# Cross-attention on one core: how Wq and Wk reach TensorE, and when x is loaded

## The chip, the core and the metric

The kernel runs on one core of a Trainium2 chip. The core has five engines that run side by side and wait for one another through semaphores: TensorE (PE in the profile, its weight loads PEld), VectorE (DVE), ScalarE (ACT), GpSimd (POOL) and SyncE (SP), which here issues every DMA. TensorE reads SBUF and writes PSUM, which has eight banks; VectorE and ScalarE copy results from PSUM to SBUF. The metric is device time in microseconds (us), as the median of the runs.

## The reference

One cross-attention layer with a residual and a layer norm. x is 16 x 256 x 256, the context c is 16 x 77 x 192; there are 8 heads of 256.

```
Q = (x @ Wq).reshape(B, -1, H, D).transpose(0, 2, 1, 3)     # Wq: 256 x 2048
K = (c @ Wk).reshape(B, -1, H, D).transpose(0, 2, 1, 3)     # Wk: 192 x 2048
V = (c @ Wv).reshape(B, -1, H, D).transpose(0, 2, 1, 3)     # Wv: 192 x 2048
score = jnp.einsum('bhqd,bhkd->bhqk', Q, K) / math.sqrt(D)
score = jnp.where(mask, score, -jnp.inf)
attn = jax.nn.softmax(score, axis=-1)
ctx = jnp.einsum('bhqk,bhkd->bqhd', attn, V).reshape(B, -1, H * D)
out = ctx @ Wo + x                                          # Wo: 2048 x 256
mu, var = mean and variance of out over its last axis
return (out - mu) * jax.lax.rsqrt(var + EPS) * gamma + beta
```

All of it is float32.

## The kernel before, in words

The weights of each head are multiplied with each other first, so that Q, K and V are never formed. For head h, G_h = Wk_h Wq_h^T / sqrt(D) is 192 x 256 (tiles gA for the first 128 rows, gB for the last 64), and U_h = Wv_h Wo_h is 192 x 256 (uA, uB). Then, for a group of four batches, A = G_h^T c^T (tile a, 256 x 77 for each head and batch), scores are x A, and for a batch V' = c U_h (tile vw, with the last 13 keys in vr). The keys are cut at 64 and 77.

The order on every engine is the order of the text: nothing is reordered by a planner. There are two stages.

The *opening* (lines 430 to 622) runs once, in this order on TensorE:

- `keep_busy(10)`: idle transposes of the identity.
- the c rows are turned by TensorE (line 475, tile pc), evicted by ACT and DVE to cA and cB; POOL doubles cB's half (line 486) and makes cRA, cRB, then clears vr (487 to 490).
- for each head, `turn_qk` turns its columns of Wq (two chunks of 128 rows) and Wk (two chunks of 96 rows) by four TensorE transposes each (line 507, tiles p_wqT and p_wkT), so that the head dimension lies on partitions; ACT evicts the one, DVE the other.
- pg (line 543) is a head's G for the first 128 rows, ph (line 524) a pair's last 64 rows, two heads side by side in the array.
- `prepare_a(0, ...)` makes A of the first group in two halves of four heads: part_A (line 182) with gA and cA, part_B (line 196) with gB and cB. Its eight banks are evicted by ACT and DVE in turn. After each half DVE turns two of the four wvT tiles by blocks of 32 x 32 (line 568).
- pu and pw (584, 602) make U, with two 64-row halves of the array at once; ACT and DVE evict, POOL copies uB's other half (613).
- pr (256, 266) makes the last keys' values; DVE turns the first group's xT; POOL turns the mask into bias (572, 618).

The loads go out in one queue on SP, in the order of the text: c in three pieces, then for each head 1-kB pieces of Wq and of Wk, then Wv in sixteen pieces of 96 KB (blocks: 32 rows on 32 partitions), Wo, the mask, xT of the first group (x in blocks), then x itself, all four groups of 1 MB (line 129; tile xg, in memory that the turned weights held before), gamma and beta. At most eight loads are under way: a load waits for the eighth before it. Any load waits in this queue behind the ones before it.

The *loop* (633 to 685) has one pass per batch: scores (295), mask and softmax on DVE, POOL and ACT, vw of the next batch (223, 234), a quarter of A of the next group (182, 196), attend (360), and finish, which adds x (372), takes the statistics and normalises; the result is stored from xg. At the first pass of a group `load_xT` loads x in blocks for the next group.

Of the kernel before, what the change touches and what calls it, by code (L numbers as in the profile page):

```python
# [15 lines left out]
P = 128  # L16
# [28 lines left out]
def kernel(  # L45
# [16 lines left out]
    LP = DL // 2  # L62
# [34 lines left out]
    gA = const.tile([P, H, DI], F32, tag="gA", name="gA")  # L97
    gB = const.tile([P, NF, DI], F32, tag="gB", name="gB")
# [66 lines left out]
    def prepare_a(g, pairs, B_first=False):  # L165


        if 0 in pairs:
            a_of[g] = in_two("a", [P, 2, GB, H, S2], g)
        parts = [(2 * n + i, dc) for n in pairs for dc in range(2) for i in range(2)]  # L170
# [19 lines left out]
        def part_B():  # L190
            if B_first:
                banks.extend(ring_of(parts))
            for j in range(0, len(parts), 2):
                for i in range(NM):
                    for k, (h, dc) in enumerate(parts[j : j + 2]):
                        nc.tensor.matmul(  # L196
                            flat(banks[j + k][i * BK : (i + 1) * BK]),
                            gB[half(k), h // 2, cols(dc, i)],
# [233 lines left out]
    with tc.tile_pool(name="wonce", bufs=1) as wp:  # L432
        c_sb = wp.tile([CR, NCR, DL], F32, tag="c", name="c_sb")
        wq_r = wq.rearrange("(t p) f -> p t f", p=P)
        wk_r = wk.rearrange("(t p) f -> p t f", p=LP)

        warm = wp.tile([P, 1], F32, tag="warm", name="warm")
        nc.scalar.activation(warm, eps, AF.Exp)
        wq_all = wp.tile([P, NF, 2, 2 * D], F32, tag="w128", name="wq_all")
        wk_all = wp.tile([LP, NF, 2, 2 * D], F32, tag="w96", name="wk_all")  # L440
        for lo, hi in ((0, 2), (2, 6), (6, NCR)):
            nc.sync.dma_start(c_sb[:, lo:hi, :], c_rows[:, lo:hi, :])
        for h in range(H):
            here, cols = slice(h % 2 * D, (h % 2 + 1) * D), slice(h * D, (h + 1) * D)
            nc.sync.dma_start(wq_all[:, h // 2, :, here], wq_r[:, :, cols])
            nc.sync.dma_start(wk_all[:, h // 2, :, here], wk_r[:, :, cols])

        wvT = wp.tile([P, NF, NL, P], F32, tag="wvT", name="wvT")
        wo_all = wp.tile([P, NF, 4, DI], F32, tag="w128", name="wo_all")
        wv_blocks = wv.rearrange("(m r) (a i f) -> a i r m f", r=BK, a=NF, i=NM)  # L450
        wo_rows = wo.rearrange("(a p n) f -> a p n f", p=P, n=4)
        for a in range(NF):
            for i in range(NM):
                nc.sync.dma_start(wvT[i * BK : (i + 1) * BK, a], wv_blocks[a, i])
        for a in range(NF):
            nc.sync.dma_start(wo_all[:, a], wo_rows[a])
# [12 lines left out]
        keep_busy(10)  # L469
        for r in range(0, NCR, 2):  # L470
            n = min(2, NCR - r)
            pc = ps_mm.tile([P, 4, P], F32, tag="mm", name=f"pc_{r}")
            for lc in range(2):
                for j in range(n):
                    nc.tensor.transpose(  # L475
                        pc[:, 2 * lc + j, :CR],
                        c_sb[:, r + j, lc * LB : lc * LB + P],
                        ident[:CR, :CR],
                    )
            rows = slice(r * CR, (r + n) * CR)  # L480
            evacuate(flat(cA)[:, rows].rearrange("p (j m) -> p j m", m=CR), pc[:, :n, :CR])
            evacuate(
                flat(cB)[LB:, rows].rearrange("p (j m) -> p j m", m=CR),
                pc[LB:, 2 : 2 + n, :CR],
            )
            nc.gpsimd.tensor_copy(flat(cB)[:LB, rows], flat(cB)[LB:, rows])
        nc.gpsimd.tensor_copy(cRA, cA[:, :, KM:])
        nc.gpsimd.tensor_copy(cRB, cB[:, :, KM:])

        nc.gpsimd.memset(vr, 0.0)  # L490


        wqT_of = [
            const.tile([P, H // 2, 2, DI], F32, tag=f"xg{i}", name=f"wqT_{i}") for i in range(2)
        ]
        wkT_of = [
            const.tile([P, H // 2, 2, DL], F32, tag=f"xg{i + 2}", name=f"wkT_{i}") for i in range(2)
        ]
        wqT = [wqT_of[h * 2 // H][:, h % (H // 2)] for h in range(H)]
        wkT = [wkT_of[h * 2 // H][:, h % (H // 2)] for h in range(H)]  # L500

        def turn_weight(dst, w_all, rows, h, tag):
            pt = ps_mm.tile([P, 4, P], F32, tag="mm", name=f"p_{tag}_{h}")
            for dc in range(2):
                for r in range(2):
                    lo = h % 2 * D + dc * P
# [222 lines left out]
```

## Time and profile before

| | us |
|---|---|
| median of 3 runs | 288.12 (287.86 to 289.52) |
| the profiled execution | 290.4 |
| its span, first to last instruction | 288.2 |
| opening, until the first scores | 61.5 |
| first pu matmul starts | 41.0 |
| TensorE busy | 277.7 (96%) |
| VectorE busy | 212.9 (74%) |
| GpSimd, ScalarE busy | 119.3, 118.5 (41% each) |
| bytes moved by DMA | 22.5 MB |

The span is the profiled execution without what lies before its first and after its last instruction, here 2.2 us. TensorE's busy time counts a matmul from its start to a modelled end. PEclk is the clock that TensorE was granted, as a share of its full speed. A group's row gives its line, engine and operation, what it writes and reads, its shape, how many there were, busy time and mean duration of one. In the chain of work, a row is when a piece starts, how long it lasts and what it is. One float32 matmul counts as two in the trace, a transpose as one.

### The profile page before, as it was taken

The numbers are of one execution on the slowest core, as the hardware profiler recorded it, in microseconds if no ns is written. First come the engines' busy times: TensorE is split into PE (matmuls) and PEld (weight loads), VectorE is DVE, ScalarE is ACT, GpSimd is POOL, SyncE is SP. The second block draws the span as 40 slices with busy tenths as digits, with TensorE's granted clock in tenths as the row PEclk, the third lists the DMA queues.
The fourth block names the chain that finished last, engine by engine and source line by source line (L and its number), as shares of the span: only waits on it lengthen the run. The fifth ranks groups of instructions, "written<-read, shape, count | busy, mean of one in ns | idle before, by whom it ended". The sixth has DMA issues, their size and how long they took to land.

```text
span 288.2 us, 11524 instructions
## 1 busy us (share of the span) xinstructions
PE 277.7 (96%) x5216; PEld 182.9 (63%) x5216; DVE 212.9 (74%) x419; ACT 118.5 (41%) x205; POOL 119.3 (41%) x150
## 2 busy tenths in 40 slices
PE   5999999999999999999999999999999999999990
PEld 5877569994757575757575757475757467575550
DVE  1322383755858798989797989897979898898884
ACT  3343221122353535353535353535353525635541
POOL 2700050705443424253434252534342518658484
PEclk9799999999999999999999999999999999999997
DMA  7998998991000100900000009000001010010112
GB/s 198 242 227 182 349 194 235 342 179 15 5 3 2 37 8 30 156 28 13 25 20 23 18 18 166 17 30 9 32 8 36 5 37 9 32 41 3 39 37 74
DMA packets 34673, 22.50 MB, mean 78 GB/s; under 512 B 17648, under 2 KB 33984, under 8 KB 34624
## 3 DMA queue, kind: packets, MB, share of 16 engines
q1 hardware_dynamic: 34624, 21.77, 32.6%
q8 instruction: 41, 0.67, 1.0%
q14 instruction: 8, 0.07, 0.1%
HBM read 17.57 MB, written 4.19 MB: 76 GB/s over the span
## 4 chain that ended last, share of the span: by engine, by line
PE 92%; DMA 2%; DVE 2%; POOL 2%; issue 1%; ACT 0%; POOLq 0%; SPq 0%
PE ps L295 23%; PE po L360 22%; PE pa L182 12%; PE pv L223 10%; PE pa L196 6%; PE pv L234 6%; PE pu L584 3%; PE pg L543 2%; PE pr L256 2%; DMA c_sb<-in_ctx_dram 2%; PE p_wqT L507 2%; PE ph L524 1%; PE pw L602 1%; PE p_wkT L507 1%; PE pr L266 1%; PE pc L475 1%
## 5 line engine op out<-in xcount | busy, mean ns | idle before, releaser
L317 POOL TENSOR_TENSOR s<-s,top 128x616 f32<-128x616 f32 x32 | 38.9, 1217 | 90.9 <-DVE top L316 86.4
L295 PE MATMUL ps<-a,xT 128*32 128x154 f32 x2048 | 70.0, 294 | 0.0
L295 PEld LDWEIGHTS ps<-a,xT 128*32 128x32 f32 x2048 | 66.4, 110 | 3.5 <-issue 0.7
L338 POOL TENSOR_TENSOR p<-e,rden 128x512 f32<-128x512 f32 x64 | 50.1, 802 | 31.8 <-ACT a L667 27.0
L360 PE MATMUL po<-vw,pT 128*32 128x256 f32 x1024 | 61.5, 380 | 0.0
L360 PEld LDWEIGHTS po<-vw,pT 128*32 128x32 f32 x1024 | 31.8, 110 | 28.2 <-issue 5.5
L330 DVE TENSOR_REDUCE den<-e 128x8 f32<-128x616 f32 x32 | 25.3, 790 | 23.6 <-ACT e L324 23.6
L182 PE MATMUL pa<-cA,gA 128*32 128x308 f32 x512 | 35.8, 423 | 0.0
L324 ACT ACTIVATE e<-s 128x616 f32<-128x616 f32 x32 | 23.0, 719 | 28.7 <-POOL s L317 28.7
L665 ACT COPY vw<-pv 128x512 f32<-128x512 f32 x32 | 18.6, 581 | 36.2 <-PE pv L234 36.2
L309 DVE TENSOR_TENSOR s<-ps,bias 128x308 f32<-128x308 f32 x64 | 27.8, 466 | 4.1 <-PE ps L295 4.1
L223 PE MATMUL pv<-uA,cA 128*32 128x512 f32 x256 | 30.4, 592 | 0.0
L182 PEld LDWEIGHTS pa<-cA,gA 128*32 128x32 f32 x512 | 16.4, 110 | 21.0 <-issue 6.6
L417 DVE SCALAR_TENSOR_TENSOR xg<-xg,rstd,bet 128x256 f32<-128x256 f32 x25 | 27.9, 1116 | 0.9
L385 ACT ACTIVATE std<-mv,eps 128x2 f32<-128x2 f32 (+1 forms) x17 | 5.0, 296 | 55.0 <-DVE mv L377 54.3
L348 DVE STREAM_TRANSPOSE pT<-p 128x640 f32<-128x640 f32 x32 | 25.0, 810 | 2.5 <-POOL p L338 2.5
L316 DVE TENSOR_REDUCE top<-s 128x8 f32<-128x616 f32 x32 | 25.5, 796 | 1.1
L360 PE MATMUL po<-vr,pT 128*32 128x256 f32 x256 | 19.7, 379 | 0.0
L385 ACT ACT_TABLE_LOAD x15 | 19.2, 1283 | 0.3
L196 PE MATMUL pa<-cB,gB 64*32 64x308 f32 x512 | 19.3, 419 | 0.0
L324 ACT ACT_TABLE_LOAD x14 | 18.0, 1283 | 0.2
L234 PE MATMUL pv<-uB,cB 64*32 64x512 f32 x256 | 17.4, 601 | 0.0
(73 smaller groups left out, 282.0 us busy)
## 6 DMA issues: line engine op xcount, KB each, us to landing
xT<-in_x_dram SPq DMA_DIRECT2D x16, 256.0 KB, 7.4
xg<-in_x_dram SPq DMA_DIRECT2D x4, 1024.0 KB, 11.4
out_dram<-xg SPq DMA_DIRECT2D x15, 256.0 KB, 2.2
wq_all<-in_L_xattn_Wq_dram SPq DMA_DIRECT2D x8, 256.0 KB, 7.7
wo_all<-in_L_xattn_Wo_dram SPq DMA_DIRECT2D x4, 512.0 KB, 5.8
wk_all<-in_L_xattn_Wk_dram SPq DMA_DIRECT2D x8, 192.0 KB, 7.7
wvT<-in_L_xattn_Wv_dram SPq DMA_DIRECT2D x16, 96.0 KB, 3.7
bias<-in_mask_BxS_if_dram SPq DMA_DIRECT2D x1, 616.0 KB, 9.3
```

Of the source, the lines that this page charges most:

```text
L182: nc.tensor.matmul(flat(o[i * BK : (i + 1) * BK]), gA[:, h, cols(dc, i)], flat(cA[:, batches, :]), start=not B_first, stop=B_first,)
L196: nc.tensor.matmul(flat(banks[j + k][i * BK : (i + 1) * BK]), gB[half(k), h // 2, cols(dc, i)], flat(cB[half(k), batches, :]), start=B_fir ...
L223: nc.tensor.matmul(pv[k][i * BK : (i + 1) * BK], cA[:, b, k * BK : (k + 1) * BK], uA[:, :, :, i], start=True, stop=False,)
L234: nc.tensor.matmul(pv[k][i * BK : (i + 1) * BK], cB[half(k), b, k * BK : (k + 1) * BK], uB[half(k), :, :, i], start=False, stop=True,)
L295: nc.tensor.matmul(ps[m // 2][i * BK : (i + 1) * BK, m % 2 * 2 * S2 : (m % 2 + 1) * 2 * S2], xT_of[g][:, j * NM + m, dc], flat(a_of[g][:, ...
L309: nc.vector.tensor_tensor(s[:, a * H // 2 : (a + 1) * H // 2], ps[a][:, : H // 2 * S2].rearrange("p (h k) -> p h k", k=S2), bias[:, b, :]. ...
L316: nc.vector.tensor_reduce(top, s, AX.X, ALU.max)
L317: nc.gpsimd.tensor_tensor(s, s, top.unsqueeze(2).to_broadcast([P, H, S2]), ALU.subtract)
L324: nc.scalar.activation(e, s_of.pop(t), AF.Exp)
L338: nc.gpsimd.tensor_tensor(part, e_mh[:, :, :, keys], rden_mh.unsqueeze(3).to_broadcast(list(part.shape)), ALU.mult,)
L360: nc.tensor.matmul(po[i * BK : (i + 1) * BK], pT[:, n, i], vw_of[b][:, n // 2, n % 2, :] if n < NF else vr[:, b, :], start=(n == 0), stop= ...
L417: nc.vector.scalar_tensor_tensor(y, y, rstd, bet, ALU.mult, ALU.add)
```

## The change

Heads are taken by two numbers: head = 2a + half in pairs before, and now place u (0 to 3) and e (0 or 1), head = u + 4e.

1. The first load is no longer c. Wq and Wk of the heads with u = 0 and 1 are loaded in pieces of 2 kB (two heads of a row), on all 128 partitions: Wk's first 128 rows for e = 0, its last 64 rows as 128 half rows, Wq for e = 0, then Wk and Wq for e = 1. They are turned by TensorE, in sets of four 128 x 128 transposes.
2. Then come three of the eleven c row sets (`first`), and the other four heads (u = 2 and 3) in blocks: each load puts 32 rows on 32 partitions in pieces of 512 bytes, as was done for Wv. VectorE turns these by 32 x 32 blocks (`turn_blk`), and G for them is made with `of_pair` and `rest_of_pairs`, the functions that pu and pw now use too.
3. A of the first group is made in two parts with G of the block heads between: places 0 and 1 after the first G, places 2 and 3 after the second. The remaining c rows are loaded after the blocks and turned after A; so POOL's cRA, cRB and vr come later too.
4. DVE turns three of the wvT tiles before the second part's copies of A and the last after them.
5. x of a group is loaded in the loop, right behind xT of that group; only x(0) is loaded in the opening, together with gamma and beta.
6. Fourteen idle transposes at the start, and two and three more between the first sets. Wo has two tiles; the second lies in wq_nat's memory, the first in its own.

```diff
-    def prepare_a(g, pairs, B_first=False):
-        if 0 in pairs:
...
-                            gB[half(k), h // 2, cols(dc, i)],
+                            gB[half(k), h % NF, cols(dc, i)],
...
-        wq_r = wq.rearrange("(t p) f -> p t f", p=P)
-        wk_r = wk.rearrange("(t p) f -> p t f", p=LP)
...
+        wq_nat = wp.tile([P, 2, 2, 2 * D], F32, tag="w128", name="wq_nat")
+        wk_nat = wp.tile([P, 2, 2 * D], F32, tag="wk", name="wk_nat")
+        wk_last = wp.tile([P, 2 * D], F32, tag="wl", name="wk_last")
...
+        wq_blk = wp.tile([P, 2, DI // BK, P], F32, tag="wqb", name="wq_blk")
+        wk_blk = wp.tile([P, 2, NL, P], F32, tag="wkb", name="wk_blk")
+        wq_blocks = wq.rearrange("(m r) (a i f) -> a i r m f", r=BK, a=NF, i=NM)
...
+        wq_rows = wq.rearrange("(t p) (e f) -> e p t f", p=P, e=2)
+        wk_rows = wk[:P].rearrange("p (e f) -> e p f", e=2)
+        wk_ends = wk[P:].rearrange("r (e f) -> (r e) f", e=2)
...
+        def load_blocks(to, blocks):
+            for i in range(NM):
+                nc.sync.dma_start(to[i * BK : (i + 1) * BK], blocks[i])
+        def load_c(lo, hi):
+            nc.sync.dma_start(c_sb[:, lo:hi, :], c_rows[:, lo:hi, :])
+        first = -(-GB * S2 // CR)
+        nc.sync.dma_start(wk_nat[:, 0], wk_rows[0][:, : 2 * D])
+        nc.sync.dma_start(wk_last, wk_ends[:, : 2 * D])
+        nc.sync.dma_start(wq_nat[:, 0], wq_rows[0][:, :, : 2 * D])
+        nc.sync.dma_start(wk_nat[:, 1], wk_rows[1][:, : 2 * D])
+        nc.sync.dma_start(wq_nat[:, 1], wq_rows[1][:, :, : 2 * D])
+        load_c(0, first)
+        for e in range(2):
+            load_blocks(wk_blk[:, e], wk_blocks[2 * e + 1])
+            load_blocks(wq_blk[:, e], wq_blocks[2 * e + 1])
+        load_c(first, NCR)
...
-        wq_all = wp.tile([P, NF, 2, 2 * D], F32, tag="w128", name="wq_all")
-        wk_all = wp.tile([LP, NF, 2, 2 * D], F32, tag="w96", name="wk_all")
-        for lo, hi in ((0, 2), (2, 6), (6, NCR)):
-            nc.sync.dma_start(c_sb[:, lo:hi, :], c_rows[:, lo:hi, :])
-        for h in range(H):
-            here, cols = slice(h % 2 * D, (h % 2 + 1) * D), slice(h * D, (h + 1) * D)
-            nc.sync.dma_start(wq_all[:, h // 2, :, here], wq_r[:, :, cols])
-            nc.sync.dma_start(wk_all[:, h // 2, :, here], wk_r[:, :, cols])
...
+        wo_of = [
+            wp.tile([P, 2, 4, DI], F32, tag=tag, name=f"wo_{i}") for i, tag in enumerate(("wo", "w128"))
+        ]
...
-            for i in range(NM):
-                nc.sync.dma_start(wvT[i * BK : (i + 1) * BK, a], wv_blocks[a, i])
+            load_blocks(wvT[:, a], wv_blocks[a])
         for a in range(NF):
-            nc.sync.dma_start(wo_all[:, a], wo_rows[a])
+            nc.sync.dma_start(wo_of[a // 2][:, a % 2], wo_rows[a])
...
-        keep_busy(10)
...
+        keep_busy(14)
...
+        qT = const.tile([P, 2, 2, 2, DI], F32, tag="xg0", name="qT")
+        kT = const.tile([P, 2, 2, 2, DL], F32, tag="xg2", name="kT")
+        qT_blk = const.tile([P, 2, 4, DI], F32, tag="xg1", name="qT_blk")
+        kT_blk = const.tile([P, 2, 4, DL], F32, tag="xg3", name="kT_blk")
...
+        def turn_q(e, u):
+            chunks = [
+                wq_nat[:, e, t, u * D + dc * P : u * D + (dc + 1) * P]
+                for dc in range(2) for t in range(2)
+            ]
+            pt = turn_chunks(chunks, f"q_{e}_{u}")
+            evacuate(flat(qT[:, e, u]), flat(pt))
+        def turn_k(e):
+            pt = turn_chunks([wk_nat[:, e, n * P : (n + 1) * P] for n in range(4)], f"k_{e}")
             evacuate(
-                flat(cB)[LB:, rows].rearrange("p (j m) -> p j m", m=CR),
-                pc[LB:, 2 : 2 + n, :CR],
+                kT[:, e].rearrange("p u n l -> p (u n) l")[:, :, :P], pt
             )
...
+        def turn_k_last():
+            pt = turn_chunks([wk_last[:, n * P : (n + 1) * P] for n in range(4)], "kl")
+            for e in range(2):
+                evacuate(
+                    kT[:, e].rearrange("p u n l -> p (u n) l")[:, :, P:],
+                    pt.rearrange("p n (r e) -> p e n r", e=2)[:, e],
+                )
+        def turn_blk(e):
+            for blk, of in ((wk_blk, kT_blk), (wq_blk, qT_blk)):
+                nc.vector.transpose(
+                    of[:, e].rearrange("p n (m r) -> p m n r", r=BK),
+                    blk[:, e].rearrange("p m (n c) -> p m n c", c=BK),
+                )
+        def turn_c(lo, hi):
...
+                nc.gpsimd.tensor_copy(flat(cB)[:LB, rows], flat(cB)[LB:, rows])
...
+        def of_pair(out, a, weight, moving):
...
             for n in range(4):
                 for e in range(2):
                     nc.tensor.matmul(
-                        pu[e][:, a % 2, :],
-                        wv_part(a, e, n)[:, :P],
-                        wo_all[half(e), a, n, :],
+                        out[e][:, a % 2, :],
+                        weight(a, e, n)[:, :P],
+                        moving(a, e, n),
                         start=(n == 0),
                         stop=(n == 3),
                     )
...
+        def rest_of_pairs(j, pairs, weight, moving, name):
+            banks = [ps_mm.tile([P, DI], F32, tag="mm", name=f"{name}_{j}_{e}") for e in range(2)]
             for n in range(4):
-                for i in range(2):
+                for i, a in enumerate(pairs):
                     for e in range(2):
                         nc.tensor.matmul(
-                            pw[e][half(i)],
-                            wv_part(pair + i, e, n)[:, P:],
-                            wo_all[half(e), pair + i, n, :],
+                            banks[e][half(i)],
+                            weight(a, e, n)[:, P:],
+                            moving(a, e, n),
                             start=(n == 0),
                             stop=(n == 3),
                         )
+            return banks
...
+        def wq_part(a, e, n):
+            return qT_blk[half(e), a, n]
+        def wk_part(a, e, n):
+            return kT_blk[half(e), a, n]
...
+        def g_of(e):
...
+            pg = ps_mm.tile([P, 2, DI], F32, tag="mm", name=f"pg_{e}")
+            for u in range(2):
+                for dc in range(2):
+                    nc.tensor.matmul(
+                        pg[:, u],
+                        kT[:, e, u, dc, :P],
+                        qT[:, e, u, dc],
+                        start=(dc == 0),
+                        stop=(dc == 1),
+                    )
+            nc.scalar.mul(gA[:, NF * e : NF * e + 2], pg, D ** -0.5)
...
+        def a_of_places(places, between=None):
+            part_A, part_B, copies = prepare_a(0, places)
+            part_A()
+            part_B()
+            for i, (dst, src) in enumerate(copies()):
+                evacuate(dst, src)
+                if between and i == 3:
+                    between()
+        turn_k(0)
+        keep_busy(2)
+        turn_k_last()
+        keep_busy(3)
+        turn_q(0, 0)
+        turn_q(0, 1)
+        g_of(0)
+        turn_k(1)
+        turn_q(1, 0)
+        turn_q(1, 1)
+        g_of(1)
+        rest_of_g(0)
+        rest_of_g(1)
+        turn_c(0, first)
+        turn_blk(0)
+        a_of_places((0, 1), lambda: turn_blk(1))
+        pg = two_banks("pgb", 0)
+        for e in range(2):
+            of_pair(pg, e, wk_part, wq_part)
+        for i in range(2):
+            nc.scalar.mul(gA.rearrange("p (e u) d -> p u e d", e=2)[:, 2 + i], pg[i], D ** -0.5)
+        for i, ph in enumerate(rest_of_pairs(0, (0, 1), wk_part, wq_part, "phb")):
+            nc.vector.tensor_scalar(gB[:, 2 + i, :], ph, D ** -0.5, None, ALU.mult)
+        for a in range(3):
+            turn_v(a)
+        load_x(0)
+        nc.sync.dma_start(gam, gamma.partition_broadcast(P))
+        nc.sync.dma_start(bet, beta.partition_broadcast(P))
+        a_of_places((2, 3))
+        turn_v(3)
+        turn_c(first, NCR)
+        nc.gpsimd.tensor_copy(cRA, cA[:, :, KM:])
+        nc.gpsimd.tensor_copy(cRB, cB[:, :, KM:])
+        nc.gpsimd.memset(vr, 0.0)
...
-        for g in range(NG):
-            load_x(g)
-            if g == 0:
-                nc.sync.dma_start(gam, gamma.partition_broadcast(P))
-                nc.sync.dma_start(bet, beta.partition_broadcast(P))
-        for n in range(0, NF, 2):
-            part_A, part_B, copies = prepare_a(0, (n, n + 1), B_first=(n > 0))
-            for part in (part_A, part_B)[:: -1 if n else 1]:
-                part()
-            for dst, src in copies():
-                evacuate(dst, src)
-            for a in range(n, n + 2):
-                blocks = wvT[:, a].rearrange("p m (c n) -> p m n c", n=4)
-                nc.vector.transpose(blocks, blocks)
...
@@ -654,6 +740,7 @@
             work.append(prepare_a(g, (n,)))
             if n == 0:
                 load_xT(g)
+                load_x(g)
```

The turned weights lie in the memory of x: qT in that of xg0, qT_blk in xg1, kT in xg2, kT_blk in xg3.

## The prediction

> **What bounds the kernel now.** I read the page's busy shares first, then the chain of work that ended last, then the stretches of the opening, then the groups for durations. Busy shares and granted clock, from the page:
>
> ```profile
> PE 277.7 (96%) x5216; PEld 182.9 (63%) x5216; DVE 212.9 (74%) x419; ACT 118.5 (41%) x205; POOL 119.3 (41%) x150
> ```
>
> TensorE is busy almost throughout. The chain in order of time (start, length, what) says whether it ever waits:
>
> ```profile
> 1.66 5.46 DMA c_sb<-in_ctx_dram
> ...
> 7.17 1.62 PE pc L475 x10
> 8.79 0.85 PE p_wqT L507 x4
> ...
> 16.38 0.45 PE p_wqT L507 x4
> 16.83 0.07 issue
> 16.89 0.52 PE p_wkT L507 x4
> 17.41 0.89 PE pg L543 x4
> 18.31 1.88 PE ph L524 x16
> ...
> 28.15 4.28 PE pa L182 x64
> 32.43 4.31 PE pa L196 x128
> 36.74 4.28 PE pa L182 x64
> 41.02 7.77 PE pu L584 x64
> ```
>
> From 7.17 on the chain is TensorE work, unbroken to 271. After 61.5 come the loop passes (14.49 us each while A is made for a later group, 11.37 after that), whose work on TensorE the change leaves alone. So I need one number: when the first pu matmul starts, 41.02 now. Busy times by stretch (start:end, length, PE busy, PEld, DVE, ACT, POOL, granted clock, DMA share, GB/s):
>
> ```profile
> 6.00:8.00 2.00, 0.83 (x7) 0.84 (x8) 0.61 (x2) 0.38 (x2) 0.74 (x2) 0.94 1.08 262
> 8.00:10.00 2.00, 2.00 (x13) 1.99 (x11) 0.98 (x3) 1.07 (x4) 1.02 (x4) 0.50 1.12 242
> 12.00:14.00 2.00, 1.96 (x14) 1.60 (x13) 0.67 (x2) 0.58 (x1) 2.00 (x1) 1.00 1.13 238
> 24.00:28.00 4.00, 4.00 (x29) 2.60 (x27) 0.98 (x2) 1.36 (x3) 0.00 (x0) 1.00 0.61 165
> ```
>
> Two things: the weights arrive at 238 to 242 GB/s, and the clock is halved around 9 us, after the 1.37 us gap before 7.17.
>
> **What goes from TensorE.** Full-clock costs are the chain's: a 128-row Wq set of four transposes 0.45, a 96-row Wk set 0.33, one head's pg 0.89, four pairs of ph 3.76. Before: transposes 8x(0.45+0.33)=6.24, pg 8x0.89=7.12, ph 3.76. After: natural transposes 4 sets of Wq and 3 of Wk (two plus the last rows), all of 128 columns, 7x0.45=3.15; pg of four heads 3.56, ph 1.88; the other four heads as of_pair on two 64-row halves at once. Those have pu's shape: 7.77/4=1.94 a pair, 3.88; their rest has pw's (chain: 3.67 for four pairs), 1.84. Total 17.12 becomes 14.31: 2.8 us less work. The rest of the gain must come from waits and the half clock: before spends 28.15-8.79=19.36 on those 17.12.
>
> **The opening, rebuilt.** Nothing of c is needed now before the weights. Bytes start to move near 2.1 (first issue 0.72). Landing lags moving: c's 0.95 MB had landed at 7.12, when the stretch 0 to 7.2 had moved 198x7.2=1.43 MB. I take 0.45 MB of lag at 1-kB pieces, somewhat less early. The first three loads, 1.05 MB, free the first turn_q. The 2-kB strided piece is in no row; bounds are 240 GB/s (1-kB pieces of the same rows) and 394 (4-kB pieces of Wo, stretch 32 to 36); nearest is the first, I take 300. With 1.4 MB moved: 2.1+1.4/0.3 = 6.8, say 7.0 (6.0 to 7.8). Before that TensorE has 14 idle transposes at 0.22 (ends 4.4) and then 5 idle and 8 real ones at 0.11: done near 5.9, so the nine added idle ones cost nothing unless the load lands before that. From T=7.0: two Wq sets 0.9, wait for the second copy 0.55 (a 512-column eviction is 0.58 on ACT, 0.69 on DVE), pg 1.78, Wk set 0.45: T+3.7. The second half of Wq (1.84 MB landed, 2.3 moved: 9.8) is there by then, so TensorE sets the pace. Two sets 0.9, wait 0.4, pg 1.78, ph 1.88, six c transposes 0.6, their copies 0.5 (0.35 and 0.25 on ACT), first A 4.28+2.15, pgb and phb 5.72, second A 6.43, the other sixteen c transposes 1.6 (four of 96 columns are 0.33, of 128 columns 0.45, so 0.4 at 112): 26.2. Sum: pu starts at 7.0+3.7+26.2=36.9, 4.1 earlier.
>
> **What must hide beside it.** *VectorE's block turns.* Two per half, 768 and 1024 columns. Two rows bound them: pT (whole 32-column blocks moved, as here) 128x640 in 0.81, so 2.3 us a half; wvT, interleaved by four, 128x768 in 1.63, so 3.8. I take the first. The first half runs from T+10, beside A's 6.4; the second is queued after four of A's eight copies, near T+15.6, ends T+17.9 and is wanted at T+18.1 by pgb's second pair (by the wvT price 1.3 us of stall). Behind it on VectorE stand two copies of A, whose banks are wanted 3 us later: nothing. *Landing of the blocks.* Sixteen loads of 96 and 128 KB, 1.84 MB. Here the Trainium skill speaks against the change: "DMA: Bandwidth & Descriptors", Rules for kernel authors, asks for at least 1 MiB a load, and its Bandwidth section gives 138 GB/s at 64 KB. By that figure they take 13.3 us after the c rows (landed near 11.5), the second half lands near 24.8, is turned at 27.1 and wanted at 25.1: 2 us of stall. The row that resembles them is Wv, the same 512-byte pieces in 96-KB loads: 3.7 us to landing with eight in flight, 8x98 kB/3.7 = 212 GB/s. By it 8.7 us: landed near 20.2, VectorE free for it at 22.6. I go by the row, the same pieces and sizes. *Queues.* SP issues 23 loads ahead of Wv where it issued 19, 0.3 to 0.5 us each, faster than they land; bytes ahead of Wo are the same, so Wo lands no later than now. The second Wo tile waits for TensorE's last read of wq_nat, 15 us earlier than SP gets there. x(1) to x(3) go onto SP behind xT of their group, 1.76 us of issue each; only stores stand behind them, and those wait 187 us for DVE anyway; each is needed four passes (58 us) later against 11.4 to land. Without that cover one wait would show in DVE's first addition. *DVE and POOL behind A.* turn_c's rest now follows turn_v(3), and VectorE has from 28.9 on two gB 0.85, three wvT turns 4.9, four copies of A 1.9, the fourth turn 1.6, four cB 1.6: until 39.8. POOL's last cB copy, cRA, cRB (0.37 each), vr memset 3.51 and bias 4.38 follow and end near 48.8. The six uB copies that pr's second part needs (0.40 each) then end near 51.2; TensorE wants them at 36.9+7.77+3.67+3.01=51.35. A tie; between 0 and 1 us I charge 0.2. ACT has room.
>
> **The clock.** The new opening leans on transposes to keep the clock up. The skill's "TensorE: Matmul & The Clock Gate", Part 4, says that transposes don't raise it. By that rule pg of the first four heads and the sets between run at half speed, some 2.5 us more, and the gain is 1.5. The trace contradicts it: the ten opening transposes go at 0.22 us each (1.34 to 3.53), the eight c ones at 4.81 at about 0.1, with no other matmul before. So transposes do raise it here, and the gap before 7.17 took it away again: by one-microsecond stretches (0.88 from 7, 0.92 from 11) the half clock lasted from 7.76 to 11.16, and in the 3.4 us before it TensorE was busy for 1.6. In the new opening that stretch holds 2.3 us of work, with a gap of about 1 us. Whether that suffices no row tells: a half clock there costs 1.4 (in before it hid behind the weights, which paced TensorE until 16.89).
>
> **The sum.** 288.2-4.1+0.2=284.3 of span. The profiled execution took 290.4, 2.2 outside the span: 286.4 for one like it. The runs' median is 288.12, close to the span itself: 284.2. One per cent, 2.9 us, is about what can be told from no change here, since repeats differ by 0.6%.
>
> **The rivals.**
> A. As summed, clock kept: 284.2 (283.2 to 285.8 by the bounds of landing and of the tie on POOL). Chance 0.52.
> B. The clock drops in the opening: the gap of about 1 us and the row at 8 to 10 speak for it, the higher busy share against: 4.1-0.2-1.4, 285.6. Chance 0.26.
> C. The blocks or the block turns come late (the 138 GB/s, the wvT price): 1.3 to 3.3 us of stall before pgb's second pair, 285.5 to 287.5. Chance 0.12.
> D. Slower: the first five loads. All take 2 kB out of every 8-kB row, and if such pieces draw on few of memory's channels at a time, the second Wq half decides in place of TensorE. From T4, its landing, pu is 26.2 away; equal to now at T4=14.8, which is 2.3 MB in 12.7 us, 180 GB/s; at 145 GB/s T4 is 18 and the time 291.3. For it: the strided 1-kB pieces got 240 where 4-kB ones got 394. Against: the same rows never fell below 199 in stretches that were not starved of issues. Chance 0.07.
> E. The loop gives it back (x loads against xT and stores): DMA share there is 0.16, so 0.03, near 288.
>
> **How the numbers follow.** A's time is the prediction. 282.8 to 286.9 holds A, B and most of C. Under 285.2 is faster by over 1%: most of A (0.49), two fifths of B (0.10), little of C (0.03): 0.62. Within: 0.31, with E. Slower, from D: 0.07.
>
> **What would show it.** Right: first pu matmul near 37; no DMA wait before TensorE after the second Wq half; idle before pgb's second pair under 0.3; block turns 1.0 and 1.3 us; loop passes still 14.49; granted clock 1.0 from about 4. Wrong: first turn_q later than 8, a clock of 0.5 near 8 to 11, wk_blk or wq_blk as releaser of DVE with pgb waiting for it, POOL's uB holding pr by more than 1 us.

## The result, and the profile after

| | before | after |
|---|---|---|
| median of 20 runs | 289.35 (287.86 to 292.71) | 286.38 (285.98 to 289.17) |
| median span of the runs | 287.2 (32 runs beside the first experiments) | 284.6 (20 runs) |
| outside the span, median | 2.15 | 1.79 |
| the profiled execution, its span | 290.4, 288.2 | 285.98, 284.2 |
| first pu matmul starts | 41.02 | 36.82 |
| from there to the end of the span | 247.2 | 247.4 |

The kernel became faster by 0.9%: the ratio is 0.991, with a 95% interval of 0.9893 to 0.9928. Ratios here leave out the runs that are over 1.5% longer than the fastest of their kernel, and they are not the quotient of the two medians, which is 0.990. The gain is clear of noise; the one per cent that the prediction took as its bound lies inside the interval. The forecast was 284.2, in a range of 282.8 to 286.9. The range holds the result; the number is 2.2 us too low, and case A's own range (to 285.8) misses the result by 0.6.

The three runs that the prediction started from (289.52, 287.86 and 288.12) are the first three of these 20; their median, 288.12, lies 1.2 us below that of all 20.

Busy times, from the page of the changed kernel:

```profile
PE 274.4 (97%) x5221; PEld 180.2 (63%) x5221; DVE 215.3 (76%) x421; ACT 115.2 (41%) x199; POOL 119.1 (42%) x150
```

TensorE is busy for 3.3 us less than in the profiled execution before, VectorE for 2.4 us more. The chain of work of the changed kernel, in order of time (start, length, what):

```profile
1.34 3.25 PE idle L493 x14
4.59 0.85 PE pt_k L507 x4
...
5.74 0.43 PE pt_kl L507 x4
6.17 0.33 PE idle L493 x3
6.50 0.62 PE pt_q L507 x4
...
7.98 1.96 PE pg L611 x8
9.94 0.44 PE pt_k L507 x4
10.38 0.45 PE pt_q L507 x4
...
16.49 4.35 PE pa L184 x64
20.84 2.23 PE pa L198 x64
23.08 3.65 PE pgb L568 x32
...
35.14 1.68 PE pc L545 x16
36.82 7.77 PE pu L568 x64
```

No DMA is in it: TensorE begins the first Wq sets at 6.50, goes into the second half's at 10.38 (that half had landed at 10.04), runs without a pause from A (16.49) through the block heads' G (pgb) and the second A, and starts pu at 36.82. The forecast was 36.9. Before, this was 41.02.

Four stretches of the opening (start:end, length, PE, PEld, DVE, ACT, POOL, granted clock, DMA share, GB/s):

```profile
6.00:8.00 2.00, 1.56 (x14) 1.17 (x12) 1.12 (x2) 0.86 (x3) 0.00 (x0) 1.00 0.98 321
8.00:10.00 2.00, 2.00 (x11) 1.75 (x11) 0.00 (x0) 0.18 (x2) 0.00 (x0) 1.00 1.18 247
12.00:14.00 2.00, 2.00 (x13) 1.40 (x14) 0.00 (x0) 0.48 (x1) 0.00 (x0) 1.00 0.98 195
18.00:20.00 2.00, 2.00 (x36) 1.03 (x32) 1.03 (x1) 0.00 (x0) 0.00 (x0) 1.00 1.06 240
```

Between 6 and 8 the 2-kB pieces arrive at 321 GB/s, where the old order had 262; the blocks come at 195 to 240 later. The clock at 8 to 10, which was 0.50, is 1.00. (A row prints 1.00 also for the time before a trace's first record of the clock, which lies at 5.46 us here and at 4.34 in the profile before. In that time the speed has to be read from the transposes: 0.22 us each at first, 0.11 from 5.74 on.)

The two closest waits of the changed kernel, from its timeline (start, length, engine, line, operation, in brackets an engine's idle time and what released it):

```profile
23.46 1.20 DVE L534 STREAM_TRANSPOSE qT_blk<-wq_blk 128x1024 f32<-128x1024 f32 x1
...
47.82 3.57 POOL L699 COPY uB<-uB 64x256 f32<-64x256 f32 x8
```

VectorE's last block turn ends at 24.66, and pgb's second pair follows the first (1.83 us from 23.08) at 24.9: it was in time by 0.2 us. POOL's eight uB copies are done at 51.4, the sixth some 0.9 earlier, and pr's second part starts right behind its first at 51.28. Neither held TensorE.

### The profile page after: what moved, and what is told of

The parts are those of the page before. It is cut to its first block, busy times and chain, and to the rows that moved or that the text cites. A ratio compares the mean times of both kernels' runs of the same rounds, so it can differ in the third digit from the quotient of the medians.

```text
span 284.2 us, 11523 instructions
## 1 busy us (share of the span) xinstructions
PE 274.4 (97%) x5221; PEld 180.2 (63%) x5221; DVE 215.3 (76%) x421; ACT 115.2 (41%) x199; POOL 119.1 (42%) x150
## 4 chain that ended last, share of the span: by engine, by line
PE 93%; DVE 2%; POOL 1%; ACT 1%; issue 1%; POOLq 0%
PE ps L297 24%; PE po L362 22%; PE pa L184 12%; PE pv L225 10%; PE pa L198 6%; PE pv L236 6%; PE pu L568 3%; PE pr L258 2%; PE pg L611 1%; PE idle L493 1%; PE pw L582 1%; PE pgb L568 1%; PE pr L268 1%; PE pc L545 1%; PE phb L582 1%; PE ph L625 1%
```

## The experiments

Each kernel was run beside the kernel before on one chip; "ratio" is its time over that of the kernel before, with the 95% interval. All compute the whole result.

### Is 41.02 the usual start of pu? The kernel before once more

The 8.8 us in which TensorE wasn't at work before pu (41.02 less 32.26 of c transposes, G and A) were read from one execution, whose time was 2.3 us above the median given. This run changes nothing.

> The kernel before, unchanged, to see span and clock of each of its runs. The two profiled spans differ by 4.0 us, the medians by 3.0. Theory 1 (landing): the weights pace TensorE until 16.9 us, landing varies, so spans spread over 2 us or more without following the clock. Theory 2 (clock): the half clock after the first gap costs 1 to 2 us, so runs with a mean clock near 0.987 are longer than those near 0.995 by about that. Either way the median of the spans should be near 287.4, 1 us below the profiled 288.2.

Measured: 289.21 (288.58 to 291.19, 14 runs), ratio 1.0 (0.9983 to 1.0018); the spans of the 14 runs go from 286.4 to 289.0. The profiled one has 286.8, 1.4 less than the execution in the prediction. Its chain:

```profile
3.74 6.60 DMA wk_all<-in_L_xattn_Wk_dram
...
10.47 0.52 PE p_wkT L507 x4
...
16.86 1.88 PE ph L524 x16
...
39.58 7.77 PE pu L584 x64
```

and the stretch from 12 to 14:

```profile
12.00:14.00 2.00, 2.00 (x18) 1.85 (x17) 0.56 (x1) 1.01 (x2) 1.56 (x1) 1.00 1.12 280
```

Here the weights come at 280 GB/s where the prediction's execution had 238. From 10.47 on TensorE isn't waiting for them any more, and pu starts at 39.58. In the other execution it was paced by arrival until 16.89. So 1.4 us of the time that the prediction counted on belongs to that execution and not to every one. The clock differs too: it was at 0.50 from 7.75 to 11.16 in that execution, and here it is at 1.00 from 4.92 on. Which of the two made the difference, this run can't say; the idle transposes below bear on it. The mean clock of a run doesn't tell long runs from short ones (a span of 286.4 has 0.997, one of 289.0 has 0.996, one of 286.5 has 0.992), but that is weak evidence, because the mean counts the time before the first record as full speed.

### Is 36.82 the usual start? The changed kernel once more

Nothing is altered: the comparison needs a second execution on both sides.

> The changed kernel once more, nothing in it altered. The kernel before was profiled twice and its pu started at 41.02 in one execution and at 39.58 in the other; the changed kernel's 36.82 is from one execution only, so the comparison of the two is lopsided until it has a second one. Theory (the gain is the 2.9 us of work taken from TensorE, and the changed kernel doesn't wait for arrival, since TensorE sets its pace from the first Wq half on): ratio to the kernel before again 0.990 to 0.992, the time 286.2 to 286.7, pu within 0.4 us of 36.8 and TensorE not at work on turns, G and A for 7.2 to 7.8 us before it. Rival (the first execution was a lucky one: the first Wq half can land at 7 to 7.7 in this order of loads too, as it did in the kernels with other orders, and the clock then drops): pu at 37.5 to 39, the ratio 0.993 to 0.996, and the spread as wide as without the idle transposes, 286 to 291.

Measured: 286.72 (285.82 to 289.86, 12 runs), ratio 0.9918 (0.9889 to 0.9947). The ratio is the theory's, the profiled execution is the rival's: it took 288.25, the tenth of the twelve, with a span of 286.5. Its chain:

```profile
2.61 9.39 DMA wq_nat<-in_L_xattn_Wq_dram
...
12.04 0.67 PE pt_q L507 x4
...
39.04 7.77 PE pu L568 x64
```

and the stretch in which TensorE waits for the second Wq half:

```profile
10.00:12.00 2.00, 0.88 (x7) 0.54 (x5) 0.69 (x1) 0.60 (x1) 0.00 (x0) 1.00 1.23 140
```

The first half is used at 6.94 and the second only at 12.04, where the execution above had 6.50 and 10.38; 140 GB/s arrive between 10 and 12, though the DMA engines are busy (share 1.23), and TensorE works for 0.88 of these two microseconds. Why that half came late isn't shown. So the changed kernel waits for weights too, in some executions, and one profile of each kernel can't say which waits the change removed. The spans of all runs can, since what follows the start of pu is the same length in all four profiles: 247.2 and 247.2 before, 247.4 and 247.5 after. Taken from the median spans, pu starts at 287.2 - 247.2 = 40.0 in the usual execution before, and at 284.6 - 247.4 = 37.2 after. From this second set it is 37.5 after (median span 284.95), and 39.8 in the kernel before beside it (median span 287.0). That estimate is used below.

### Was it the clock or the arrival? Idle transposes in the opening before

Before the first weights TensorE waited 1.37 us and then worked at half clock. This kernel fills the wait.

```diff
             nc.gpsimd.tensor_copy(flat(cB)[:LB, rows], flat(cB)[LB:, rows])
+            keep_busy({0: 3, 4: 12}.get(r, 0))
```

> The kernel before with idle transposes in the two gaps of the c transposes (three after the first pair of row sets, twelve after the third), so that TensorE is busy from 1.3 us on. Theory 1 (landing): the clock stays full near 8 to 11 us, and pu starts within 0.3 us of where it does in the kernel before on the same chip, since the weights' landing decides until 16.9; median within 0.5 us. Theory 2 (clock): 1 to 2 us faster and a narrower spread.

Measured: 289.09 (288.54 to 290.88, 14 runs), ratio 0.9991 (0.9972 to 1.001). pu starts at 40.18 in its profile. The fill was worth nothing that can be measured: the half clock near 9 us, which one of the two profiles of the kernel before has and the other has not, shows no price.

### Are 2-kB pieces enough? Only the load sizes changed

Wq and Wk as before in order and turns, but loaded for two heads at a time, in 2-kB pieces.

```diff
-        for h in range(H):
-            here, cols = slice(h % 2 * D, (h % 2 + 1) * D), slice(h * D, (h + 1) * D)
-            nc.sync.dma_start(wq_all[:, h // 2, :, here], wq_r[:, :, cols])
-            nc.sync.dma_start(wk_all[:, h // 2, :, here], wk_r[:, :, cols])
+        for n in range(NF):
+            cols = slice(2 * n * D, 2 * (n + 1) * D)
+            nc.sync.dma_start(wq_all[:, n], wq_r[:, :, cols])
+            nc.sync.dma_start(wk_all[:, n], wk_r[:, :, cols])
```

> The kernel before with Wq and Wk loaded by pairs of heads, in 2-kB pieces (eight loads in place of sixteen), nothing else. Theory: the weights move at about 300 GB/s in place of 240, the last is there near 19.5 in place of 22.9, TensorE is paced by them only up to the first pair (near 10.3) and pu starts near 40.0, 0.6 to 1.0 us earlier. Rival (pieces don't matter, the order and VectorE's turns do): no change or, as the first head now waits for a pair, up to 1 us slower.

Measured: 293.02 (292.32 to 293.63, 4 runs), ratio 1.0128 (1.0103 to 1.0153): slower by 3.7 us. Both theories fell. The chain of this kernel:

```profile
2.73 7.90 DMA wk_all<-in_L_xattn_Wk_dram
...
10.77 0.87 PE p_wkT L507 x4
...
13.13 1.76 PE pg L543 x4
...
18.29 0.89 PE pg L543 x4
```

and, from its timeline, the c transposes ahead of the weights:

```profile
5.12 3.85 PE L475 MATMUL pc<-ident,c_sb 112*128 112x112 f32 x18 [0.63 <-DMA c_sb<-in_ctx_dram]
```

The pieces arrived at 273 to 330 GB/s between 6 and 16 us, the 1-kB pieces in the second profile of the kernel before at 271 to 289: hardly faster. The first head is now complete only with the second one's bytes (Wk at 10.63). But most of the loss is the clock, which had not come up at all: the c transposes already take 0.21 us each, pg of a head takes 1.76 us at 13.13 and 0.89 at 18.29, and the trace's first record of the clock, at full speed, is at 16.74. From 10.77 until then TensorE works without a pause at half speed, so some 3 of these 6 us are lost, by estimate. pu starts at 44.10 in this profile. So this kernel is a loss, but it doesn't say what 2-kB pieces are worth at full clock: that was not tried.

### Is the order alone the gain? c behind the weights in the kernel before

```diff
-        for lo, hi in ((0, 2), (2, 6), (6, NCR)):
-            nc.sync.dma_start(c_sb[:, lo:hi, :], c_rows[:, lo:hi, :])
...
             nc.sync.dma_start(wk_all[:, h // 2, :, here], wk_r[:, :, cols])
+        for lo, hi in ((0, 2), (2, 6), (6, NCR)):
+            nc.sync.dma_start(c_sb[:, lo:hi, :], c_rows[:, lo:hi, :])
```

The c turns stand behind the last G.

> The kernel before with one part of the change alone: c is loaded behind the weights and turned by TensorE after the last head's G; heads, pieces and turns as before. Theory (the gain is start plus less TensorE work): TensorE begins its heads near 4.3 in place of 9 to 10.5, weights arrive at about the pace it uses them, pu starts near 38, 1.5 us earlier than in the kernel before and 1.2 later than in the changed kernel; time 287.5 to 288.3. Rival (only VectorE's share of the turns counts): no change against the kernel before. Rival (start is all): within 0.4 us of the changed kernel.

Measured: 289.71 (288.3 to 291.82, 14 runs), ratio 1.0004 (0.9978 to 1.0031), pu at 41.59 in the profile. The theory fell; what was measured is its first rival, no change. From its chain:

```profile
8.30 1.76 PE pg L520 x4
...
14.06 0.89 PE pg L520 x4
```

The heads begin early, but with short waits between them, and TensorE works at half speed until 13.15, where the trace has its first record of the clock: what the early start gains, the clock takes. So I gave the same kernel idle transposes as the changed kernel has them (14 at the start, some between the first two heads' sets):

```diff
-        keep_busy(10)
+        keep_busy(14)
...
             turn_weight(wqT[h], wq_all, P, h, "wqT")
+            keep_busy({0: 2, 1: 8}.get(h, 0))
             turn_weight(wkT[h], wk_all, LP, h, "wkT")
+            keep_busy({0: 4}.get(h, 0))
```

> As the kernel with c behind the weights, which started TensorE at 3.8 and yet gained nothing, since its clock stayed at half until 13.2; now with fourteen idle transposes at the start and two, four and eight in the waits of the first two heads, so that TensorE is never idle. Theory (start and clock together make the gain): full clock from about 5 or 6, heads paced by their weights, last G near 22, c turned by 24.3, pu near 37.5 to 38.5, time 286.5 to 288. Rival (the weights' landing decides in this order, whatever the clock): pu stays near 41, time near 289.5.

Measured: 289.02 (288.45 to 289.66, 22 runs), ratio 0.9987 (0.9974 to 0.9999). The chain:

```profile
7.90 0.88 PE idle L467 x8
...
9.11 0.89 PE pg L522 x4
...
39.96 7.77 PE pu L585 x64
```

The clock is full at 9.11, TensorE runs unbroken to pu, and pu still starts at 39.96 (and the 22 runs lie close together). Little of that is due to the idle transposes: the fifth head's Wk landed at 13.29 and was turned at 13.76, so in this execution TensorE could have been 0.5 us earlier at most, with pu at 39.5; the usual execution of the changed kernel has 37.2 to 37.5. The theory that early start and full clock make the gain fell. What these kernels lack is the other part of the change: they do 17.1 us of turns and G on TensorE, the changed kernel 14.1, and the whole difference is transposes (3.1 us at full clock, where eight heads took 6.2). Half the heads turned on VectorE, with blocks that land and turn beside A, is what is left to account for the gain. That part was not tried alone, so this is an argument by what is left over.

### How close are the block turns? A behind both of them, and turns done twice

First kernel: the second block turn and pgb stand ahead of the first half of A, so that A no longer covers the blocks' landing.

```diff
         turn_blk(0)
-        a_of_places((0, 1), lambda: turn_blk(1))
+        turn_blk(1)
...
-        a_of_places((2, 3))
+        a_of_places((0, 1))
+        a_of_places((2, 3))
         turn_v(3)
```

> The changed kernel without A between: both block turns and both G first, then all of A. Theory: TensorE reaches pgb near 16, its first pair's turn ends near 19, the second half lands near 20 and is turned near 22.3, so pgb ends near 24.2 where it could have ended at 19.7; pu starts 3.6 to 4.5 us later than in the changed kernel, near 41, and all of the gain is gone. Rival (blocks are there early enough anyway): less than 1 us.

Second kernel: VectorE does each block turn twice.

```diff
-            for blk, of in ((wk_blk, kT_blk), (wq_blk, qT_blk)):
+            for blk, of in ((wk_blk, kT_blk), (wq_blk, qT_blk)) * 2:
```

> The changed kernel with every block turn of VectorE done twice. The second half's turns begin at 22.6 and take 4.3 in place of 2.1 us, so end near 26.9, and pgb's second pair wants them at 24.8. Theory (the turns are hidden with 0.2 us to spare): pgb stalls 2.1 us, pu starts near 38.9, 2.1 us longer (up to 1.7 more if the wait halves the clock). Rival (VectorE has room): under 0.5 us.

Measured: the first 291.22 (289.7 to 294.52, 11 runs; 290.95 without the two longest), ratio 1.0056 (1.0035 to 1.0077), 4.2 to 4.6 us above the two medians of the changed kernel; the second 289.01 (287.99 to 292.12, 22 runs), ratio 0.9988 (0.9968 to 1.0009), 2.3 to 2.6 us above them. From the chain of the first:

```profile
18.03 1.21 DVE qT_blk L534
...
19.37 5.41 PE pgb L568 x32
```

its clock after the wait:

```profile
20.00:22.00 2.00, 2.00 (x12) 1.89 (x10) 1.21 (x2) 0.00 (x0) 0.00 (x0) 0.50 1.17 237
```

and from the timeline of the second:

```profile
25.99 1.20 DVE L534 STREAM_TRANSPOSE qT_blk<-wq_blk 128x1024 f32<-128x1024 f32 x1
...
27.24 2.00 PE L568 MATMUL pgb<-qT_blk,kT_blk 64*128 64x256 f32 x16 [1.65 <-DVE qT_blk L534]
```

In the first, pgb waits for VectorE until 19.37 (3.1 us of idle time in the timeline) and then takes 5.41 us instead of 3.65, since the clock is at 0.50 for 3.41 us from 19.41 on. A between the halves is worth more than the wait that it covers. In the second, TensorE waits 1.65 us for the last turn, which ends at 27.2 instead of 24.7. (The rest of the 2.3 to 2.6 is not this wait: in this profile A had already begun 0.5 us later than in the changed kernel's first.) The second half's turns take 2.1 us longer, so by this wait VectorE had some 0.4 us in hand, and 0.2 by the changed kernel's profile: its turn is on the edge of the path, as the prediction had it.

### What are the idle transposes worth?

```diff
-        keep_busy(14)
+        keep_busy(10)
...
         turn_k(0)
-        keep_busy(2)
         turn_k_last()
-        keep_busy(3)
         turn_q(0, 0)
```

> The changed kernel with ten idle transposes at the start and none between the first sets. Theory (clock): TensorE then has a gap of 1 to 2 us before the first Wq set, the clock reaches full speed later than 5.5 us in some executions, and the sets and pg after it run at half speed for up to 3.4 us: median 0.5 to 2 us longer than the changed kernel, wider spread. Rival (the idle transposes don't matter): within 0.3 us, same spread.

Measured: 287.95 (286.05 to 291.2, 18 runs; 287.84 without the three longest), ratio 0.9926 (0.9898 to 0.9954). That is 1.1 to 1.5 us above the two medians of the changed kernel, but the intervals of the ratios overlap: whether the idle transposes pay is not settled by these runs. The chain and one line of the timeline show what they are against:

```profile
3.88 1.12 PE L507 MATMUL pt_k<-ident,wk_nat 128*128 128x128 f32 x4
...
7.78 1.97 PE pt_q L507 x8
9.77 2.54 PE pg L611 x8
...
39.19 7.77 PE pu L568 x64
```

In this execution the first Wq half landed at 7.73. TensorE had waited 1.72 us for it, and then worked at half clock, which isn't the wait's doing alone: the clock had not come up before it either (four transposes took 1.12 us at 3.88), and its first record is at 10.95. The two sets took 1.97 us where 0.9 is full speed, and pg 2.54 instead of 1.96, some 1.6 us together. So rival B is a real mechanism, and it comes where the opening is left idle.

### Does the place of the x loads matter?

All four x loads in the opening, as before, none in the loop.

```diff
-        load_x(0)
+        for g in range(NG):
+            load_x(g)
...
                 load_xT(g)
-                load_x(g)
```

> The changed kernel with x of all four groups loaded in the opening, as before, in place of a group ahead in the loop. Theory (transfers are off the path): span and time within 0.3 us of the changed kernel. Rival (part of the gain is that 3 MB less move between 43 and 60 us): up to 1 us longer.

Measured: 286.63 (286.09 to 290.24, 9 runs), ratio 0.9924 (0.9884 to 0.9964), span 284.7 in the profile: no difference from the changed kernel. That part of the change is neutral, within the 0.4% that these nine runs can tell.

### Does the first Wq half land earlier with fewer bytes ahead of it?

Two kernels move `wk_last`: in the first it is loaded and turned behind the first Wq half (with seven idle transposes in place of the two and three), in the second it changes places with the second Wk piece.

```diff
-        nc.sync.dma_start(wk_last, wk_ends[:, : 2 * D])
         nc.sync.dma_start(wq_nat[:, 0], wq_rows[0][:, :, : 2 * D])
+        nc.sync.dma_start(wk_last, wk_ends[:, : 2 * D])
```

> The changed kernel with the last rows of Wk loaded and turned after the first half of Wq, so that only 0.79 MB stand before the first Wq set. Theory (the first megabyte's landing decides, then TensorE): the first Wq set starts near 5.7 in place of 6.45, the second half of Wq (landed near 10.0) becomes the limit, pu starts 0.3 us earlier. Rival (TensorE's earlier pace decides): no change.

```diff
-        nc.sync.dma_start(wk_last, wk_ends[:, : 2 * D])
+        nc.sync.dma_start(wk_nat[:, 1], wk_rows[1][:, : 2 * D])
         nc.sync.dma_start(wq_nat[:, 0], wq_rows[0][:, :, : 2 * D])
-        nc.sync.dma_start(wk_nat[:, 1], wk_rows[1][:, : 2 * D])
+        nc.sync.dma_start(wk_last, wk_ends[:, : 2 * D])
```

> The changed kernel with Wk's second half loaded and turned second, in place of Wk's last rows, which come fourth; as many bytes stand before the first Wq set as in the changed kernel. In the kernel with the last rows third, Wq's first half came right behind Wk's first half, all from the same 4 kB of every 8-kB row, and landed at 6.95 with fewer bytes before it than in the changed kernel (6.4). Theory (loads that draw on the same half of the rows hinder each other): with the other half between them Wq lands near 6.4 and the time is that of the changed kernel. Rival (Wk's last rows, half the rows and both halves of each, must be among the first): Wq lands at 7 or later and the time is 0.7 us longer.

Measured: 287.09 (286.89 to 287.55, 6 runs), ratio 0.9906 (0.9878 to 0.9935), and 287.03 (286.58 to 289.15, 11 runs), ratio 0.9929 (0.9903 to 0.9954). In the profiles the first Wq half landed at 6.95 and 7.38, against 6.4 in the changed kernel's first profile, and 216 and 224 GB/s arrived between 4 and 6 us, against 316. Taken alone that would say that Wk's last rows belong among the first loads. But the second profile of the changed kernel has 6.9 and 270 GB/s, and none of the ratios can be told from those of the changed kernel. So fewer bytes ahead of Wq brought nothing, and the order that was chosen isn't shown to be better either. This stays open.

## Why the prediction was right or wrong

**The path, right for a good execution.** The prediction built the start of pu as 7.0+3.7+26.2=36.9. The first profile has 6.4 (the first Wq half is there) plus 4.0 to the second half's sets (10.38) plus 26.4: 36.82. Its span is the shortest of its 20 runs; in the usual execution pu is at 37.2 to 37.5, so the match to a tenth is luck. The second profile has 6.9 plus 5.1 plus 27.0: 39.04 (of the 0.6 in the last term, pgb took 0.35, with a pause after its first eight matmuls). The link that gave way there is "The second half of Wq ... is there by then, so TensorE sets the pace": forecast to land at 9.8, it landed at 10.0 in the one and at 12.0 in the other. The rest of the sum was good: G and its turns on TensorE are 14.1 us at full clock, where the forecast had 14.31, since pgb took 3.65 for 3.88 (its weight loads take 186 ns each, where those of pu, read with a stride, took 325).

**The covers, right.** The block turns took 0.97 and 1.20 us (forecast 1.0 and 1.3 by the pT row). The blocks came at 195 to 240 GB/s, 214 in the mean of the stretches from 12 to 20 (forecast 212, by Wv's row), and the last had landed at 19.98 in the first profile (forecast 20.2) and at 22.36 in the second, each before VectorE turned to it. The Trainium skill's figure in "DMA: Bandwidth & Descriptors", Bandwidth, is 138 GB/s for 64 KB issued from GpSimd; taken as a bound for these loads of 96 and 128 KB from SP, with eight under way, it fails, and rival C with it: no stall. The x loads cost nothing that shows. POOL's tie was a tie, at zero instead of 0.2: in both profiles pr goes on without a pause. Loop passes take 14.49 still.

**The clock, right.** Transposes alone did raise it: the first ones go at 0.22 us each (4.59 0.85 for four), those from 5.74 on at 0.11 (5.74 0.43 for four), and only transposes had run until then; the first record of full clock is at 5.46, where the forecast had about 4. The Trainium skill's "TensorE: Matmul & The Clock Gate", Part 4, says that the full clock doesn't engage for transposes; the measurement decides against it. (Ahead of the half clock in the kernel before TensorE was busy for 1.7 us, where the prediction read 1.6.) In both profiles of the changed kernel pg of the first two heads takes 1.96 us, near the forecast 1.78 and far from the 3.5 of half speed. Rival B stood at 0.26 and didn't come; the kernel without nine of the idle transposes shows it, though there the clock doesn't drop but comes up late.

**The time, too low by 2.2 us: the step "The runs' median is 288.12, close to the span itself: 284.2".** The span was forecast at 284.3; the profiled one is 284.2, the median of 20 runs 284.6. But the time of a run is its span and what lies outside: 1.75 to 1.93 us in the 20 runs of the changed kernel (median 1.79), and 2.15 in the median of those of before. A three-run median near the span of one profiled execution is a comparison of two different executions: a time of 288.12 with 2.15 outside has a span of 286.0, not 288.2. The sentence before it, 286.4 for one like the profiled execution (284.3 and 2.2 make 286.5), had the right form, and I went by the wrong one; that it also hits the median of 286.38 is luck, since its span is 0.3 too short and its outside 0.4 too long. Of the 2.2, 1.9 is this step and 0.3 is the span.

**The gain, too large by 1.3 to 1.8 us: the step "The rest of the gain must come from waits and the half clock: before spends 28.15-8.79=19.36 on those 17.12".** The forecast was 4.1 us of earlier pu. The first pair of profiles even has 4.2. But that pair sets a long execution of before (span 288.2, median 287.2) against the shortest of after. From the median spans pu is 2.8 earlier (40.0 to 37.2) in the first set and 2.3 (39.8 to 37.5) in the second. TensorE's work up to pu is 2.26 (c) + 17.12 + 12.87 (A) = 32.3 before, and 2.2 + 14.1 + 13.1 = 29.4 after: 2.9 less. The time in which it isn't at that work, or is slow at it, is then:

| | profile 1 | profile 2 | from the median spans |
|---|---|---|---|
| before | 8.8 | 7.3 | 7.5 to 7.7 |
| after | 7.4 | 9.6 | 7.8 to 8.1 |

So by this account the work taken from TensorE makes up the whole gain, and the waits are as long as they were, only in other places. It is bookkeeping, not an experiment: no kernel has the block turns alone. The 1.3 us of waits and half clock in the forecast belonged to one execution, with its slow arrival (238 GB/s). The runs of the kernel before agree: idle transposes, which take away the half clock alone, gained nothing, and weights first with a full clock gained 0.3.

**The remaining 0.4.** Medians differ by 2.97 us and spans by 2.6; the other 0.37 lies outside the span, before the first or after the last instruction. Every variant of the changed kernel has about 1.8 there, every variant of the kernel before about 2.15. It isn't the x loads (with all of them in the opening it is 1.79) nor the place of c (at the end it is 2.15). Its cause wasn't found.

**Chances.** The ratio misses the side with 0.62, faster by over 1%, by a tenth of a per cent, and lies in the middle, with 0.31; its interval reaches into both. With 1.79 us outside the span added as a term of its own, the same path would have given 284.3 + 1.8 = 286.1.

## What to carry to other kernels

Before counting a wait as gain, look whether a second execution of the same kernel has it; where the stretch behind it has a fixed length, the spans of all runs tell its usual size. What survives is work taken from the engine that is never idle, as long as the other engine's share fits under it; here half the heads' turns went to VectorE, with 0.2 to 0.4 us to spare. Add what lies outside the span as a term of its own, from the span and the time of the same run.

## What the runs showed of the hardware

- The cost of a wait on TensorE can be more than its length, because the clock halves: after 3.1 us of idle time ahead of pgb it was at 0.50 for 3.41 us and pgb itself took 1.8 us longer (5.41 against 3.65). The length of the wait alone doesn't decide. In the first profile of the kernel before TensorE was busy for 1.7 of the 3.41 us ahead of 7.75, and the clock fell to 0.50 for the next 3.41; in the second profile of the changed kernel it was busy for 2.25 of the 3.41 us ahead of 12.04, where it had waited 1.16 in one piece, and the clock stayed at 1.00.
- The full clock has to be reached first, and short waits can put it off. The first record of full speed is at 4.3 to 5.5 us in the two profiles each of the kernel before and the changed kernel, at 10.95 without the idle transposes, at 13.15 with c behind the weights and at 16.74 with 2-kB loads, though there TensorE was busy for 80 to 100% of the stretches from 8 to 16 us.
- The same loads arrive at a different rate from execution to execution: 238 to 242 GB/s and 280 to 299 for the 1-kB pieces of Wq and Wk in the kernel before; and in the changed kernel the second Wq half at 10.0 and at 12.0. Pieces of 2 kB out of the same 8-kB rows got 273 to 330, hardly more than those of 1 kB at their best.
